# Q, K and V by the seven-product scheme at two levels instead of one, in a two-layer graph-attention kernel

## The chip, the core and the metric

The kernel runs on one core of one Trainium2 chip. The metric is the time of one execution on the device in microseconds (us), the median of several runs. Beside it stands one profiled execution with a trace of every instruction. The engines are named as the profile names them: PE is TensorE's matmul, PEld its weight load, DVE is VectorE, ACT is ScalarE, POOL is GpSimd, SP is the engine whose queue issues nearly all transfers.

## The reference

There are 128 batches of 128 tokens with 512 features, in float32, and a 128x128 mask of zeros and ones per batch. Two layers follow one another, each inside a residual and a normalisation:

```python
q = (x @ Wq + bq), k = (x @ Wk + bk), v = (x @ Wv + bv)      # 512x512 weights, 8 heads of 64
logits = einsum(q, k) / sqrt(64);  logits = where(adj > 0, logits, -1e9)
out = relu(einsum(softmax(logits), v) @ Wo + bo)
x = layernorm(x + out)
# layer 1
Wh = x @ W;  s_i = Wh @ a1;  s_j = Wh @ a2
e = leaky(s_i[:, None] + s_j[None, :]);  e = where(adj > 0, e, -9e15)
h = leaky(softmax(e, axis=1) @ Wh)
x = layernorm(x + h)
```

The five products with 512x512 weights (Wq, Wk, Wv, Wo, W) hold most of the arithmetic.

## The kernel before

**Tiling.** Batches go in groups of four (`GROUP = 4`, 512 tokens). Q, K and V are computed for a group at a time. Wo and W are applied to pairs of batches (256 tokens). Softmax and the second layer's attention go batch by batch.

**The seven-product scheme.** A product of two matrices cut into 2x2 blocks needs eight block products; Strassen's scheme, in the variant used here, needs seven and some sums of blocks. The weights' sums are made once at the start (`right_blocks`, L152 to L155). The sums of x are made on GpSimd (`left_blocks`, L276 to L279: xS per group for Q, K and V, oS and x1S per pair for Wo and W). For Q, K and V a block is 256 tokens by 256 features, so one product of blocks is four 128x128 weight loads, each with 256 columns streamed, on L367:

```python
for m in range(2):
    cols = slice(m * P, (m + 1) * P)
    for kc in range(2):
        lhs, rhs = xs[:, kc, cols], w[:, kc, :]
        if transposed_out:
            lhs, rhs = w[:, kc, cols], xs[:, kc, :]
        nc.tensor.matmul(p[:, m, :], lhs, rhs, start=..., stop=True)
```

A float32 product on PE shows as two records in the trace. The seven products p1 to p7 of one matrix go to three PSUM banks (y, w, x; `ps_st`, one buffer each) in an order that lets later products add to what earlier ones left in a bank:

```python
ORDER = (("p1", "t0"), ("p5",), ("p6", "t2"), ("p2", "c11"),
         ("p7", "t3", "c22"), ("p4", "c21"), ("p3", "c12"))
```

p1, p6, p7 and p4 all go to bank y. After p1, p6 and p7 ACT copies that bank out (t0, t2, t3: L344, or L348 where Q's bias is added), so p6 must wait for t0, and so on. c21 is a copy by ACT too. c11, c22 and c12 are sums on DVE of a bank and a copy (L385, 512 columns). Per matrix and group that is 7 products, 4 copies and 3 sums.

**The rest.** `scores` (L520) multiplies Q and K of one batch into two banks; DVE adds the mask (L534), takes the maxima (L543); ACT takes the exponentials (L554) and divides by the sums (L568). The attention matrix goes out to DRAM in `store` and comes back as 32-row stripes in `fetch` (L581), DVE transposes it in 32x32 blocks (L587), and `attend` (L600) multiplies by V. Wo and W follow in `pair_product` (L448), with copies on ACT (L459) and sums on DVE (L693, L697, L772, and residuals on L686). Normalisations take their statistics on DVE (L644, L646), a power on GpSimd (L650, L652) and are applied on DVE (L665). The second layer's attention is one product (L841). The scores e are turned by way of DRAM, too (`store_sender`, `fetch_sender`, L817 on DVE), and its softmax is scaled on DVE (L836).

**Weights.** The seven blocks of Wq and Wk stay in SBUF. Those of Wv are written to DRAM once and fetched again in every group (`wv_n`, 256 KB a block, seven per group, three buffers).

**Order.** Everything is issued in one program order, and each engine works through its own instructions in that order. A step `t` of the main loop is one batch. Even steps start the softmax of two batches and apply W to an older pair, odd steps finish the softmax and apply Wo. Between these pieces, `group()` issues the next product of Q, K or V, and `pair()` the next of Wo or W. So the order follows from the places of these calls in the loop. The last four batches follow an order written out by hand (`PLAN`). All transfers but four go through SP's queue, which works in order as well.

Of the kernel before, what the change touches and what calls it, by code (L numbers as in the profile page):

```python
# [17 lines left out]
GROUP = 4  # L18
# [3 lines left out]


@with_exitstack
def kernel(
# [16 lines left out]

# [28 lines left out]
    b_rows = small.tile([2 * NC, P], F32, name="b_rows", tag="e", bufs=1)  # L111
    b_cols = const.tile([P, 2, NC], F32, name="b_cols")

    def turn_biases():
        p_b = psum("p_b")
        nc.tensor.transpose(p_b[:, : 2 * NC], b_rows, ident[: 2 * NC, : 2 * NC])
        nc.vector.tensor_scalar_mul(b_cols[:, 0, :], p_b[:, :NC], QSCALE)
        nc.vector.tensor_copy(b_cols[:, 1, :], p_b[:, NC : 2 * NC])

# [44 lines left out]
    wq = const.tile([P, 7, 2, HALF], F32, name="wq")  # L164
    wk = const.tile([P, 7, 2, HALF], F32, name="wk")
    wo = const.tile([P, 7, 2, HALF], F32, name="wo")
    w1 = const.tile([P, 7, 2, HALF + 1], F32, name="w1")
    wv = dram.tile([7, P, 2, HALF], F32, name="wv", bufs=1)
# [3 lines left out]

    def load_wv():

        tiles = [big.tile([P, 2, 2, HALF], F32, name="wv_t", tag="v", bufs=3) for _ in range(3)]
        tiles.append(work.tile([P, 2, 2, HALF], F32, name="wv_t", tag="pa", bufs=2))
        t = [tiles[n // 2][:, n % 2] for n in range(7)]
        load_blocks(Wv, tiles[:2], nc.sync)

        def write(n):  # L180
            return lambda: nc.sync.dma_start(wv[n], t[PLACE[n]])

        ops = right_blocks(t)
        return [write(0)] + ops + [write(n) for n in (4, 5, 1, 6, 3, 2)]
# [5 lines left out]
    def load_w1():  # L190

        a_b = [work.tile([P, D], F32, name="a_b", tag="wh", bufs=4) for _ in range(2)]
# [5 lines left out]
        loads = [load_a(0), load_a(1)] + block_loads(W1, columns(w1), nc.sync)  # L198
# [34 lines left out]
    X, XT, XS, Q, K, V, MF, OT, X1T, X1, WH = ({} for _ in range(11))  # L233


    def spread(src):

        z = work.tile([P, 4, P], F32, name="xz", bufs=3)
        block = src.rearrange("(a i) (q e) -> q i a e", i=32, q=4)
        for q in range(4):  # L240
            nc.sync.dma_start(z[32 * q : 32 * q + 32], block[q])
        return z
# [8 lines left out]
    def load_x(b):  # L251
        X[b] = spread(x[b])

    def load_residual(b):

        X1[b] = work.tile([P, D], F32, name="x1", bufs=7)
        nc.sync.dma_start(X1[b], x[b])

# [6 lines left out]
    def sum_x(g):  # L265
        sums = big.tile([P, 3, 2, 2 * P], F32, name="xS")
        XS[g], ops = left_blocks(XT[g], sums)
        return lambda: [op() for op in ops]

# [71 lines left out]
    def copy_out(dst, p, o, bias):  # L341

        if bias is None:
            nc.scalar.copy(dst, p)  # L344
            return
        for m in range(2):
            col = bias[:, 2 * o + m : 2 * o + m + 1]
            nc.scalar.activation(dst[:, m, :], p[:, m, :], AF.Identity, bias=col)  # L348

    def group_product(g, turn, weight, out, transposed_out, bias=None):  # L350

        def bank(role):

            tag = "abc"[("ywx".index(role) - turn) % 3]
            return ps_st.tile([P, 2, 2 * P], F32, name=f"st_{role}", tag=tag)

        def multiply(p, n, start):
            w, xs = weight(n), XS[g][n]  # L360
            for m in range(2):
                cols = slice(m * P, (m + 1) * P)
                for kc in range(2):
                    lhs, rhs = xs[:, kc, cols], w[:, kc, :]
                    if transposed_out:
                        lhs, rhs = w[:, kc, cols], xs[:, kc, :]
                    nc.tensor.matmul(  # L367
                        p[:, m, :],
                        lhs,
                        rhs,  # L370
                        start=start and m == 0 and kc == 0,
                        stop=True,
                        skip_group_check=True,
                    )

        def read(name, p, o):
            t = work.tile([P, 2, 2 * P], F32, name=f"st_{name}")
            copy_out(t, p, o, bias)
            return t

        def add(h, o, p, t):
            if t is None:
                copy_out(out(h, o), p, o, bias)
            else:
                nc.vector.tensor_add(out(h, o), p, t)  # L385

        return strassen(bank, multiply, read, add)

    def products(g):

        for h in range(2):
            Q[g, h] = big.tile([P, NC, HALF], F32, name="qT", bufs=4)
            K[g, h] = big.tile([P, NC, HALF], F32, name="kT", bufs=3)
            V[g, h] = big.tile([P, 2, D], F32, name="v", bufs=3)

        def features_first(dst):
            return lambda h, o: dst[g, h][:, 2 * o : 2 * o + 2, :]

        def tokens_first(dst):
            return lambda h, o: dst[g, h][:, :, o * HALF : (o + 1) * HALF]  # L400

        ring, todo = {}, [0, 4, 5, 1, 6, 3, 2]

        def fetch():
            if todo:
                n = todo.pop(0)
                ring[n] = work.tile([P, 2, HALF], F32, name="wv_n", bufs=3)
                nc.sync.dma_start(ring[n], wv[n])

        pieces = [  # L410
            group_product(g, 3 * g, lambda n: wq[:, PLACE[n]], features_first(Q), True, b_cols[:, 0, :]),
            group_product(g, 3 * g + 1, lambda n: wk[:, PLACE[n]], features_first(K), True),
            group_product(g, 3 * g + 2, ring.pop, tokens_first(V), False),
        ]

        chains = [in_order(chain) for chain in pieces]

        def with_fetch(step, n=1):
            def run():
                step()  # L420
                for _ in range(n):
                    fetch()

            return run

        chains[1][0] = with_fetch(chains[1][0], 2)
        chains[2][0] = with_fetch(chains[2][0])
        chains[1][5] = with_fetch(chains[1][5])
        for n in (1, 2, 3):
            chains[2][n] = with_fetch(chains[2][n])  # L430

        order = [chains[0][n] for n in ((0, 3, 1, 2, 4) if g == 0 else range(5))]
        if g == 0:
            first = order[0]
            order[0] = lambda: (first(), other_half())
        order += [chains[1][0], *chains[0][5:], *chains[1][1:5]]
        order += [chains[2][0], chains[1][6], chains[1][5], *chains[2][1:5]]
        return order + chains[2][5:], pieces[2], fetch
# [427 lines left out]
    def on(b):  # L866
        return 0 <= b < B
# [370 lines left out]

# [176 lines left out]
```

## Time and profile before

| | value |
|---|---|
| median of 3 runs | 2357.7 us (2355.76 to 2360.14) |
| profiled execution | 2352.5 us, span of its instructions 2350.7 us |
| granted PE clock | 0.999 |
| instructions | 43613 |
| PE / PEld busy | 2324.7 us (99%) / 1978.8 us (84%) |
| DVE busy | 1706.9 us (73%) |
| ACT busy | 1506.7 us (64%) |
| POOL busy | 763.0 us (32%) |
| transfers | 395.28 MB, mean 168 GB/s, 54.4% of 16 DMA engines' time in the main queue |

In such a profile "busy" is the time in which at least one instruction of the engine runs, as a share of the span. A matmul's end is modelled, and matmuls overlap in the pipeline, so that a busy PE is not yet one that starts a matmul as often as it can: the distance from one start to the next tells that. A group row names line, engine, operation, output<-input, shapes, count, then busy time and the mean of one instruction, then the idle time before these instructions and what ended it. A timeline row gives start and length in us, engine, line, and how many alike instructions were merged.

### The profile page before, as it was taken

Reading aid. Unit: us, or ns where it says so; the run is one execution under the profiler, and the core shown is the slowest. Engines: PE = TensorE matmul, PEld = TensorE weight load, DVE = VectorE, ACT = ScalarE, POOL = GpSimd, SP = SyncE. Lnnn points to the kernel's source line nnn. Section 1 sums busy time; section 2 is a strip of 40 time slices with the busy share of each in tenths; the row PEclk is TensorE's granted clock in tenths of the full one; section 3 lists DMA queues with packets and bytes.
Section 4 is the critical chain, followed back from the end, with each engine's and each line's share of the span. In section 5 each row is a group of like instructions: output and inputs, shape, how many; then the busy total and the mean of one; then the engine's idle time right before and its main releaser. Section 6 shows DMA issues by size and latency. Waiting matters only on the chain.

```text
span 2350.7 us, 43613 instructions
## 1 busy us (share of the span) xinstructions
PE 2324.7 (99%) x13362; PEld 1978.8 (84%) x13362; DVE 1706.9 (73%) x3462; ACT 1506.7 (64%) x5459; POOL 763.0 (32%) x1191
## 2 busy tenths in 40 slices
PE   8999999999999999999999999999999999999998
PEld 7788888888888888888888888888888888888875
DVE  5677776777767777777777677677777776777767
ACT  3656656657666666566665666665766666657676
POOL 2232333323333323333233333333332333323326
PEclk9999999999999999999999999999999999999999
DMA  7655555555555555555555555555555555555454
GB/s 198 181 167 165 167 168 173 170 160 176 169 163 175 167 172 160 170 175 162 166 169 166 178 169 164 169 171 162 174 165 169 174 161 177 166 167 169 155 166 131
DMA packets 435561, 395.28 MB, mean 168 GB/s; under 512 B 108280, under 2 KB 339328, under 8 KB 435328
## 3 DMA queue, kind: packets, MB, share of 16 engines
q1 hardware_dynamic: 435008, 392.23, 54.4%
q8 instruction: 107, 1.75, 0.3%
q14 instruction: 126, 1.03, 0.1%
q10 hardware_dynamic: 320, 0.26, 0.0%
HBM read 248.58 MB, written 143.72 MB: 167 GB/s over the span
## 4 chain that ended last, share of the span: by engine, by line
PE 92%; DMA 3%; DVE 2%; ACT 1%; SPq 1%; issue 1%; POOL 0%; POOLq 0%; DVEq 0%; ACTq 0%
PE st_y L367 26%; PE p_y L448 18%; PE st_w L367 13%; PE p_w L448 9%; PE st_x L367 7%; PE lg L520 5%; PE p_oT L600 5%; PE p_h L841 4%; PE p_x L448 4%; DMA paz<-pa_dram 1%; DMA pa_dram<-pa 1%; ACT pa L568 0%; ACT pa L554 0%; SPq L581 0%; DMA e_dram<-e 0%
## 5 line engine op out<-in xcount | busy, mean ns | idle before, releaser
L650 POOL TENSOR_SCALAR ve<-mv 128x1 f32<-128x1 f32 x256 | 70.0, 273 | 1415.4 <-DVE mv L646 1409.7
L554 ACT ACTIVATE pa<-pa,nmax 128x128 f32<-128x128 f32 x1008 | 393.5, 394 | 2.6 <-DVE nmax L543 2.6
L568 ACT ACTIVATE pa<-pa,rs 128x128 f32<-128x128 f32 x1008 | 327.6, 397 | 0.7 <-DVE rs L564 0.6
L344 ACT COPY st_t<-st_y 128x512 f32<-128x512 f32 x192 | 111.2, 579 | 198.3 <-PE st_y L367 198.0
L459 ACT COPY pr_t<-p_y 128x257 f32<-128x257 f32 (+1 forms) x375 | 139.0, 371 | 125.1 <-PE p_y L448 120.7
L348 ACT ACTIVATE st_t<-st_y,b_cols 128x256 f32<-128x256 f32 x192 | 79.8, 466 | 202.3 <-PE st_y L367 202.3
L554 ACT ACTIVATION_READ_ACCUMULATOR pa<-pa,nmax 128x1 f32 x1008 | 192.5, 191 | 0.0
L587 DVE STREAM_TRANSPOSE pa<-paz 128x1024 f32<-128x1024 f32 x126 | 156.9, 1246 | 15.7 <-DMA paz<-pa_dram 14.1
L534 DVE TENSOR_TENSOR pa<-lg,mf 128x512 f32<-128x512 f32 x252 | 161.1, 680 | 1.1 <-PE lg L520 1.1
L614 ACT ACTIVATE oT<-p_oT,b_cols 128x128 f32<-128x128 f32 x504 | 137.1, 380 | 37.4 <-PE p_oT L600 37.3
L543 DVE TENSOR_REDUCE nmax<-pa 128x8 f32<-128x1024 f32 x126 | 151.7, 1204 | 2.2
L600 PEld LDWEIGHTS p_oT<-pa,v 128*64 128x64 f32 x2016 | 108.6, 137 | 51.7 <-issue 23.7
L652 POOL TENSOR_TENSOR rstd<-ve,mhalf 128x1 f32<-128x1 f32 x256 | 144.8, 566 | 21.3
L520 PE MATMUL lg<-kT,qT 64*128 64x128 f32 x2048 | 132.1, 279 | 0.0
L448 PE MATMUL p_y<-wo,oT 128*128 128x256 f32 x504 | 129.7, 380 | 1.2 <-ACT p_y L469 1.2
L520 PEld LDWEIGHTS lg<-kT,qT 64*128 64x128 f32 x2048 | 119.4, 188 | 12.3 <-issue 11.9
L448 PE MATMUL p_y<-w,x1T 128*128 128x257 f32 x496 | 128.4, 381 | 1.3 <-ACT wk L459 1.3
L448 PE MATMUL p_y<-wo,oS 128*128 128x256 f32 x504 | 129.5, 379 | 0.1
L600 PE MATMUL p_oT<-pa,v 128*64 128x128 f32 x2016 | 125.1, 276 | 4.5 <-DVE pa L587 3.9
L448 PE MATMUL p_y<-w,x1S 128*128 128x257 f32 x496 | 127.9, 380 | 0.0
L367 PE MATMUL st_y<-xT,wk 128*128 128x256 f32 x512 | 124.0, 385 | 0.0
L367 PE MATMUL st_y<-wv_n,xT 128*128 128x256 f32 x512 | 121.3, 380 | 1.5 <-ACT st_t L344 1.4
(197 smaller groups left out, 5726.9 us busy)
## 6 DMA issues: line engine op xcount, KB each, us to landing
pa_dram<-pa SPq DMA_DIRECT2D x126, 512.0 KB, 2.9
paz<-pa_dram SPq DMA_DIRECT2D x504, 128.0 KB, 2.8
wv_n<-wv SPq DMA_DIRECT2D x224, 256.0 KB, 3.0
x<-in_x_dram SPq DMA_DIRECT2D x128, 256.0 KB, 3.0
x_dram<-x SPq DMA_DIRECT2D x128, 256.0 KB, 2.4
xz<-x_dram SPq DMA_DIRECT2D x512, 64.0 KB, 2.0
xz<-in_x_dram SPq DMA_DIRECT2D x496, 64.0 KB, 2.2
out_dram<-z SPq DMA_DIRECT2D x120, 256.0 KB, 2.7
```

The source lines that it names most:

```text
L367: nc.tensor.matmul(p[:, m, :], lhs, rhs, start=start and m == 0 and kc == 0, stop=True, skip_group_check=True,)
L448: nc.tensor.matmul(p[:, :width], xs()[n][:, kc, :], w[:, PLACE[n], kc, :], start=start and kc == 0, stop=True, skip_group_check=True,)
L459: nc.scalar.copy(t[:, :width], p[:, :width])
L520: nc.tensor.matmul(self.lg[r][:, c, :], q[rows, c, cols], k[rows, c, cols], start=c == 0, stop=True, skip_group_check=True,)
L534: nc.vector.tensor_add(by_head[:, r * NC : (r + 1) * NC], self.lg[r].rearrange("p c (b k) -> p c b k", b=4), mf.unsqueeze(1).to_broadcast( ...
L543: nc.vector.tensor_reduce(self.nmax, by_head, AX.XY, ALU.max, negate=True)
L554: nc.scalar.activation(self.pa[:, :, h, :], self.pa[:, :, h, :], AF.Exp, bias=self.nmax[:, h : h + 1], accum_out=self.sums[:, h : h + 1],)
L568: nc.scalar.activation(self.pa[:, :, h, :], self.pa[:, :, h, :], AF.Copy, scale=self.rs[:, h : h + 1])
L587: nc.vector.transpose(self.paT.rearrange("p h (a i) -> p a h i", i=32), self.paz.rearrange("p a (h k) -> p a h k", k=32),)
L600: nc.tensor.matmul(self.oT[r * HD : (r + 1) * HD, c, :], v[:, h * HD : (h + 1) * HD], self.paT[:, r * NC + c, :], start=c == 0, stop=True, ...
L614: nc.scalar.activation(OT[pair][:, c, h * P : (h + 1) * P], self.oT[:, c, :], AF.Identity, bias=b_cols[:, 1, c : c + 1],)
L652: nc.gpsimd.tensor_tensor(self.r, ve, mhalf, ALU.pow)
```

## The change

Each of the seven products of 256-wide blocks is cut again into 2x2 blocks of 128x128 and done by seven products, so that Q, K and V take 49 products of 128x128 by 128x128 each where they took 28 of 128x128 by 128x256.

The inner seven products are done in two rounds, `ROUNDS = ((0, 1, 4, 2), (5, 3, 6))`. A "chain" c is one matrix in one round: six chains per group. A chain runs the outer order p1 to p7 as before, but each outer product is now four (or three) matmuls of 128 columns, each into its own quarter of the bank. Copies and sums of the outer scheme are done on those 512 or 384 columns at once, into `out_Q`, `out_K`, `out_V` or scratch `cells`; there are twice as many of them. When both rounds are there, `combine` does the inner scheme's sums in SBUF: per group Q takes ten adds, six of them half as wide, K and V seven each. The inner sums of x (s1 to s4, each as one add of 512 and one of 384 columns) are new, too; they are made from x's outer sums once per group. Most of these adds are on GpSimd, some on DVE.

```diff
-            for m in range(2):
-                cols = slice(m * P, (m + 1) * P)
-                for kc in range(2):
-                    lhs, rhs = xs[:, kc, cols], w[:, kc, :]
-                    if transposed_out:
-                        lhs, rhs = w[:, kc, cols], xs[:, kc, :]
-                    nc.tensor.matmul(p[:, m, :], lhs, rhs, ...
+            j = place_in_stream.get((c, f"p{n + 1}"))
+            if j is not None:
+                fetch_until(j + AHEAD)
+            operand = INNER[g][1]
+            for index, m in enumerate(ROUNDS[r]):
+                xs = operand(n, INNER_PLACE.index(m))
+                w = weight(n, m)
+                lhs, rhs = (xs, w) if name == "V" else (w, xs)
+                nc.tensor.matmul(p[:, index, :], lhs, rhs, ...
...
+    def combine(c, engine):
...
+        def op(dst, left, right):
+            def run(by=None):
+                (by or engine).tensor_add(*(t(n) for t, n in (dst, left, right)))
...
+        if c % 6 == 0:
+            ops = []
+            for h, src in enumerate((half(0), raw)):
+                d, s = ([(t, n) for n in range(4)] for t in (half(h), src))
+                ops += [op(d[2], s[2], s[0]), op(d[0], s[0], s[3]), op(d[1], s[1], d[2])]
+            return ops
+        if c % 2 == 0:
+            return [op(s[2], s[2], s[0]), op(s[0], s[0], s[3]), op(s[1], s[1], s[2])]
+        return [
+            op(s[3], s[1], m[0]),
+            op(s[1], s[1], m[1]),
+            op(s[2], s[2], m[0]),
+            op(s[2], s[2], m[2]),
         ]
...
+        ops = {
+            "s1": ("tensor_add", "s1", a21, a22),
+            "s2": ("tensor_sub", "s2", "s1", a11),
+            "s3": ("tensor_sub", a21, a11, a21),
+            "s4": ("tensor_sub", "s4", a12, "s2"),
+        }
```

All 49 blocks of Wq are in SBUF. Those of Wk and Wv are made at the start (Wk's on DVE, Wv's on GpSimd), written to DRAM, and fetched in every group but the first, one or two outer products at a time, three fetches ahead, into four buffers of 512 KB:

```diff
+            blocks = work.tile([P, 2, 4, P], F32, name="w_n", bufs=AHEAD + 1)
...
+            nc.sync.dma_start(blocks[:, : len(at), : 4 - r, :], src.rearrange("n p i f -> p n i f"))
```

To make room, Wo and W lie where Wk's blocks lay at first, and x, Wh, z and oT share one tile (`arena`). Some small transfers of two batches are merged into one (x, the mask, the residual, the senders of e).

From step 6 to the last four batches the loop's calls are replaced by four lists, one per kind of step, that name every piece in order. `h` issues the next outer product of Q, K or V, `a` and `d` the next waiting copy on ACT or sum on DVE of that scheme, `k` the next add of `combine` (with `.v` on DVE), `i` an inner sum of x; w and z are the products with W and Wo, f and s the two softmaxes, e and n the second layer. One of the four, and the loop's core:

```diff
+    2: """
+        n.residual f.scores s.scores h w.p1 f.add.1 f.add.0 w.p5 f.reduce s.add.1
+        e.turn_blocks w.t0 w.p6 g.apply.0 k.v k.v f.exp.6.7 f.exp.4.5 w.t2 e.add h k.v
+        s.add.0 d f.reciprocals.1 m.turn e.maxima n.stats w.p2 n.rstd w.p7 a f.exp.0.1 w.t3
...
+            elif name == "a":
+                if acts:
+                    acts.pop(0)()
+            elif name == "d":
+                if vecs:
+                    vecs.pop(0)()
+            elif name == "k":
+                if combos:
+                    combos.pop(0)(nc.vector if rest else nc.gpsimd)
+            elif name == "i":
+                inner_sum(g if t % GROUP else g + 1, rest[0][:2], rest[0][2:],
+                          nc.vector if rest[1:] else nc.gpsimd)
```

At the start, the first product waits for a part of Wq's and x's inner differences, made on DVE (`wq.first`, `wq.second`, `x_inner`), and the other parts follow in `other_half`. At the end, two chains of V instead of one are left for the hand-written order, with their seven adds. The program's matmuls for Q, K and V go from 2688 to 4704, its DVE instructions from 3448 to 4220, its GpSimd instructions from 1196 to 1754, and SP's transfers from 3021 to 2543.

## The prediction, on record before the changed kernel was run

> **What bounds the kernel now.** I read the page from the top: busy shares, then the chain that ended last, then the stretches by time, then single lines.
>
> ```profile
> PE 2324.7 (99%) x13362; PEld 1978.8 (84%) x13362; DVE 1706.9 (73%) x3462; ACT 1506.7 (64%) x5459; POOL 763.0 (32%) x1191
> ...
> PE 92%; DMA 3%; DVE 2%; ACT 1%; SPq 1%; issue 1%; POOL 0%; POOLq 0%; DVEq 0%; ACTq 0%
> PE st_y L367 26%; PE p_y L448 18%; PE st_w L367 13%; PE p_w L448 9%; PE st_x L367 7%; PE lg L520 5%; PE p_oT L600 5%; PE p_h L841 4%; PE p_x L448 4%; DMA paz<-pa_dram 1%; DMA pa_dram<-pa 1%; ACT pa L568 0%; ACT pa L554 0%; SPq L581 0%; DMA e_dram<-e 0%
> ```
>
> TensorE bounds it, and 46% of the chain (26 + 13 + 7) is the product of L367 that the change rewrites. A busy matmul row is not yet a full one, so I check the spacing of starts in the timeline (columns: start, length in us):
>
> ```profile
> 9.85 1.04 PE L942 MATMUL p_x<-ident,x_turned 128*128 128x128 f32 x8
> 10.72 1.46 PE L367 MATMUL st_x<-xT,wq 128*128 128x256 f32 x6
> ...
> 1205.76 1.89 PE L367 MATMUL st_y<-xS,wq 128*128 128x256 f32 x8
> 1207.49 1.02 PE L841 MATMUL p_h<-wh,att 128*128 128x512 f32 x2
> ...
> 1211.33 0.86 PEld L520 LDWEIGHTS lg<-kT,qT 64*128 64x128 f32 x14
> ```
>
> Eight records of 256 columns start within 1.73 us, 216 ns each. (A product of 128x128 by 128x256 is two records: 5376 in the trace for 2688 in the program.) Eight transposes, each with its own 128x128 load and 128 columns, start within 0.87 us, 109 ns each. The last line is seven pairs of loads: (0.86 - 0.19)/6 = 112 ns per pair, two halves of 64 rows, each load 188 ns long, each followed by 128 columns.
>
> Then one group of four batches. The GpSimd sum L276, once per group, starts 24 times from 315.9 to 1974.4: 72.1 us per group. Eight groups by engine (columns: window, length, then busy PE, PEld, DVE, ACT, POOL, clock, DMA share, GB/s):
>
> ```profile
> 400.00:976.80 576.80, 576.80 (x3329) 493.40 (x3328) 423.46 (x856) 372.70 (x1361) 186.62 (x288) 1.00 0.55 169
> ```
>
> Per group: DVE 52.9, ACT 46.6, POOL 23.3 us. PE has no slack, DVE has 19 us.
>
> **What the Trainium skill says.** "TensorE: Matmul & The Clock Gate", section "LDWEIGHTS (loading the stationary operand)": the load takes columns/1.2 ns, 107 ns for 128, whatever the rows; its "Step-by-step" part says that the next load runs under the matmul in flight. The trace agrees: 84% PEld lies beside 99% PE, and the 112 ns pair fits a hidden load. The same page's "Back-to-back issue gap" has pairs at 128 columns at 81 ns where a lone gap is 56: 25 ns of load can show. No row here does so. "SBUF — State Buffer", section "SBUF: two separate sides": a DVE instruction with two SBUF inputs or in a 2-port mode and a GpSimd one hold one port pair exclusively; the loser waits. "GPSIMD Engine Reference", "Performance versus the Vector engine": a GpSimd add takes 1.96 times the DVE's; the trace has 1.27 against 0.69 us. On the lock the trace agrees:
>
> ```profile
> 1211.89 0.72 POOL L276 TENSOR_TENSOR oS<-oT 128x256 f32<-128x256 f32 x1
> ...
> 1210.66 0.52 DVE L665 TENSOR_SCALAR x<-x,mv,rstd 128x512 f32<-128x512 f32 x1
> 1211.92 0.97 DVE L665 TENSOR_SCALAR x<-x,mv,rstd 128x512 f32<-128x512 f32 x1
> ...
> 17.02 1.75 DVE L155 TENSOR_TENSOR wq<-wq 128x512 f32<-128x512 f32 x1
> 21.67 0.69 DVE L155 TENSOR_TENSOR wk<-wk 128x512 f32<-128x512 f32 x1
> ```
>
> The same DVE instruction takes 0.52 us alone and 0.97 beside a GpSimd add; a two-input add 0.69 alone and 1.75 in the start, where GpSimd sums at the same time.
>
> **The change, part by part, per group.**
>
> 1. *PE.* Removed: 3 x 28 products, 168 records at 216 ns, 36.3 us. Added: 3 x 49 products of 128 columns, 294 records at 110 ns (between 109 and 112), 32.3 us. Saved: **4.0 us**; 72.1 becomes 68.1. If 25 ns of load show, 294 x 134 = 39.4, 3.1 lost. The loads double their share: a record then has a load for each 107 ns stream. I take 110, because both rows with a load per 128 columns show it.
>
> 2. *DVE.* Each product now ends in two rounds (four and three blocks), so nine more sums out of PSUM of 384 columns come. The inner combination adds six of 512 and three of 256 on DVE, and the inner sums of x three of 512 and three of 384. 512-column adds start 0.61 us apart (21.06 to 21.67), 256 columns take 0.42 less the same overlap of 0.08, 0.34; 384 between, 0.47. Sum: 9 x 0.47 + 9 x 0.61 + 3 x 0.34 + 3 x 0.47 = **12.1 us**. DVE 65.0 of 68.1: the cover that hid all its work is almost used up.
>
> 3. *GpSimd.* Thirteen adds of 512 (12 combining, one inner sum) at 1.3, three of 256 at 0.73, one of 384 at 1.0: 20 us more, 43 of 68. It has room itself. But the lock: DVE has 39 instructions per group of the kinds named (4 residual sums of z, 8 normalisations, 4 + 4 on att and mf, 4 residuals of layer zero, 15 of the new ones), and GpSimd adds cover 36 of 68 us. Met by chance and held 0.4 us each, that is 39 x 0.54 x 0.4 = 8.4 us. Before has some of it in its 52.9: the means of 639 and 871 ns for normalisations and 543 for att, against 0.52 and 0.29 alone, make 86 us, 2.7 per group. So +5.7 by chance; from 0 (the lists place them apart) to 13 (all meet). Below zero is excluded unless meetings fall under today's. I take 3.5: DVE 68.5.
>
> 4. *ACT.* Twelve more copies of 384 columns at some 0.38 (0.371 for 256 and 0.585 for 512, less 0.1 overlap), Q's bias in smaller pieces: +4.9, 51.5 of 68. Hidden.
>
> 5. *Transfers.* K and V come from DRAM: 98 blocks of 64 KB, 6.4 MB, where V alone was 1.8; 12.2 MB per group become 16.8 and the share 0.55 some 0.78 at worst, less if the larger packets go faster. A fetch holds 512 or 384 KB, landing in perhaps twice the 3.0 us of wv_n, and is issued three fetches, some five products or 8 us, ahead: hidden. SP issues in order; a fetch behind the store of pa waits for ACT's divisions, and x, adj and paz behind a fetch wait for a free one of four buffers. SP's transfers fall from 3021 to 2543, since pairs of small loads are merged. 0 to 1.5 us per group; I take 0 and keep 1.5.
>
> 6. *Orders as lists.* Moving steps costs nothing in itself, but each engine's queue is strict: a DVE sum that waits for PE holds the sums behind it, ACT's copies of p1 and p6 free the bank that the next product of four or three short matmuls (0.9 or 0.65 us, before 1.7) wants. Two engines at about 68 us that wait for each other do not both stay full: +1.2, between 0 and 5.
>
> 7. *Start.* Inner differences of Wq and x before the first products can end: about ten adds of 0.4 to 1.0 us, beside GpSimd: +6 us, 0 to 12. The end has two chains of V instead of one; its adds lie beside softmax: 0.
>
> Period: 68.5 + 1.2 = 69.7, 2.4 less than 72.1. Sum against the profiled execution: 2352.5 (span 2350.7 and 1.8 around it) - 32 x 2.4 + 6 = 2282. The median of the runs lies 5.2 above that execution: **2287 us**.
>
> **The rivals.**
>
> - *DVE and its lock become the bound; slower.* One mechanism, in the steady groups on DVE: 65.0 + 5.7 by chance, and 3 us idle for waits on PE and ACT, make 73.7, 1.6 over today: 2357.7 + 51 + 6 = 2415 us. It decides as soon as lock and idle time together exceed 7 us per group (72.1 - 65.0). For it: the sums leave 3 us, and DVE today waits 115 us for pr_t of ACT and 67 for p_w of PE. Against it: the combining work has a whole group to be done in and may be placed where DVE reads PSUM. 28 in 100.
> - *PE gets all of it.* DVE's sums fit beside PE, the lock is met no more than now: 2357.7 - 128 + 6 = 2236 us. 15 in 100.
> - *The load shows.* With 134 ns per record 3.1 us per group are lost, 2357.7 + 99 + 6 = 2463; at the full 190 ns of a load 294 x 0.19 = 55.9, about 2990. Against: the 109 and 112 ns above. 3 in 100.
> - *Gains and losses cancel*, within 0.2% (about 5 us, what runs of this kernel can tell from no change): 4 in 100.
>
> **The numbers.** Likeliest, 50 in 100: 2287 us, by itself 2250 to 2345. Faster 0.65 (50 + 15), same 0.04, slower 0.31 (28 + 3). The range runs from the PE case with a cheap start, 2230, to the lock case, 2415; it leaves out the visible load, the worst of the lock and the best corner.
>
> **What would show it.** Right: L367's successor at 109 to 112 ns per start with PEld near the whole span; DVE over 92% busy; GpSimd near 62%; DVE's two-input adds longer in the mean than 0.69 us; PE idle before products, released by DVE and ACT; groups some 69 to 70 us apart. Wrong: matmul starts over 120 ns apart with nothing awaited (step 1); DVE under 88% busy and PE full (steps 2 and 3 too dear); waits of PE on w_n (step 5); normalisations and new adds over 1 us in the mean and groups over 72 us apart (the first rival).

## The result, and the profile after

| | before | after |
|---|---|---|
| median | 2358.75 us (4 runs, 2355.76 to 2360.14) | 2584.31 us (4 runs, 2581.41 to 2593.21) |
| span of the profiled execution | 2350.7 us | 2579.6 us |
| maxima of the third group's first batch | 168.9 us | 236.8 us |
| one group of four batches, steady | 72.1 us | 77.6 us |
| from the 29th group's maxima to the end | 309.3 us | 325.4 us |

After/before is 1.0964 (95% interval 1.0934 to 1.0995): slower, where 2287 us and a faster kernel were predicted, and beyond the range's end of 2415. The third to fifth rows are read from DVE's reduction of the logits to their maxima (`nmax`), in each group that of its first batch; the steady value is the mean over the fifth to 29th group. The 229 us between the spans are 68 in the start, 145 in the 26 groups that follow, and 16 in the end.

The page of after, busy times and the chain that ended last (shares by engine, then by line):

```profile
PE 2313.3 (90%) x17394; PEld 2035.5 (79%) x17394; DVE 2170.0 (84%) x4234; ACT 1663.7 (64%) x5971; POOL 1504.3 (58%) x1749
...
DVE 34%; DMA 28%; PE 15%; ACT 10%; SPq 7%; issue 5%; POOL 1%; DVEq 0%; ACTq 0%; POOLq 0%
```

(SPq is SP's queue issuing transfers.) PE fell from 92% of the chain to 15%. No engine took its place: DVE is busy 84%, the DMA engines about 73% (see below). The chain hops between DVE, transfers and ACT; the reading here is that the length of such a chain of steps, and not one full engine, sets the period. PE itself works at the pace that was forecast (timeline of after; start, length):

```profile
1217.60 0.39 PE L578 MATMUL st_w<-xT,wq 128*128 128x128 f32 x2
1217.82 0.39 PE L578 MATMUL st_w<-inner_s,wq 128*128 128x128 f32 x2
...
1218.49 0.61 PE L578 MATMUL st_w<-inner_s,w_n 128*128 128x128 f32 x4
```

Eight records start within 0.89 us, 111 ns each, with wq and with streamed weights alike. What PE waits for in the steady stretch, here always 400 to 2300 us, of after (total, times, longest):

```profile
PE p_oT L896 <- DVE pa L883: 45.3, 40, 3.3
PE st_y L578 <- DVE out_Q L612: 33.6, 25, 1.4
PE st_x L578 <- DMA w_n<-wk: 23.9, 20, 2.6
PE st_y L578 <- ACT cells L591: 20.3, 25, 0.8
```

In the same stretch of before the sum of all PE's waits that the trace names is under 3 us; the longest of its lines is

```profile
PE st_y L367 <- DMA wv_n<-wv: 1.1, 1, 1.1
```

The first line of after ends a round trip: pa, the attention matrix, is stored to DRAM, fetched as stripes (paz), and transposed on DVE (L883). The page's list of transfers gives its legs (KB each, median us from issue to landing), those of before first, then those of after beside the new stream:

```profile
pa_dram<-pa SPq DMA_DIRECT2D x126, 512.0 KB, 2.9
paz<-pa_dram SPq DMA_DIRECT2D x504, 128.0 KB, 2.8
```

```profile
paz<-pa_dram SPq DMA_DIRECT2D x504, 128.0 KB, 3.2
pa_dram<-pa SPq DMA_DIRECT2D x125, 512.0 KB, 4.4
w_n<-wk SPq DMA_DIRECT2D x93, 512.0 KB, 4.8
w_n<-wv SPq DMA_DIRECT2D x93, 512.0 KB, 5.7
```

A mean share hides this. The steady stretch as a whole, then slices of 4 us of after (window, length, busy PE, PEld, DVE, ACT, POOL, clock, DMA share, GB/s) and PE's timeline in them:

```profile
400.00:2300.00 1900.00, 1745.06 (x13285) 1538.32 (x13284) 1633.53 (x3220) 1263.40 (x4568) 1124.68 (x1299) 1.00 0.73 216
```

```profile
1224.00:1228.00 4.00, 4.00 (x31) 3.79 (x30) 3.03 (x6) 3.86 (x15) 1.07 (x2) 1.00 0.94 251
1228.00:1232.00 4.00, 1.42 (x13) 1.26 (x13) 1.46 (x5) 2.49 (x8) 3.84 (x5) 1.00 1.04 234
1232.00:1236.00 4.00, 4.00 (x17) 3.41 (x16) 1.66 (x3) 0.37 (x1) 1.03 (x2) 0.60 0.92 297
```
```profile
1231.57 0.46 PE L578 MATMUL st_x<-xT,w_n 128*128 128x128 f32 x2 [2.58 <-DMA w_n<-wk]
...
1233.54 1.91 PE L742 MATMUL p_w<-wo_w,oS 128*128 128x256 f32 x4
...
1238.81 1.03 PE L742 MATMUL p_w<-wo_w,arena 128*128 128x256 f32 x4
```

For 12 us the DMA engines are full while the mean over the groups is 0.73. That is no rare case: of the 475 slices of 4 us in the steady stretch, 152 have a share of 0.90 or more, against 2 in the kernel before. PE waits 2.58 us for one fetch, the longest wait of that line, and then pays again: its clock falls to 0.60, and four records that take 1.03 us at full clock take 1.91. The second payment is rare in after: the clock was at half for 10 of the 1900 us.

### The profile page after: what moved, and what is told of

The parts are those of the page before. It is cut to its first block, busy times and chain, and to the rows that moved or that the text cites. A ratio compares the mean times of both kernels' runs of the same rounds, so it can differ in the third digit from the quotient of the medians.

```text
span 2579.6 us, 53024 instructions
## 1 busy us (share of the span) xinstructions
PE 2313.3 (90%) x17394; PEld 2035.5 (79%) x17394; DVE 2170.0 (84%) x4234; ACT 1663.7 (64%) x5971; POOL 1504.3 (58%) x1749
## 3 DMA queue, kind: packets, MB, share of 16 engines
q1 hardware_dynamic: 516064, 537.17, 70.5%
## 4 chain that ended last, share of the span: by engine, by line
DVE 34%; DMA 28%; PE 15%; ACT 10%; SPq 7%; issue 5%; POOL 1%; DVEq 0%; ACTq 0%; POOLq 0%
DMA paz<-pa_dram 12%; PE st_y L578 5%; DVE pa L883 4%; SPq L877 4%; PE p_y L742 4%; DMA x_dram<-arena 3%; DMA w_n<-wk 3%; DVE pa L830 3%; ACT pa L850 3%; DMA xz<-x_dram 3%; DVE arena L962 3%; DMA pa_dram<-pa 3%; DVE out_Q L628 3%; ACT pa L864 2%; DVE nmax L839 2%
## 5 line engine op out<-in xcount | busy, mean ns | idle before, releaser
L1156 ACT ACTIVATE arena<-p_h 128x512 f32<-128x512 f32 x120 | 71.6, 597 | 271.9 <-DMA out_dram<-arena 191.9
L883 DVE STREAM_TRANSPOSE pa<-paz 128x1024 f32<-128x1024 f32 x125 | 154.8, 1239 | 100.0 <-DMA paz<-pa_dram 97.2
L591 ACT COPY cells<-st_y 128x384 f32<-128x384 f32 x288 | 136.8, 475 | 121.2 <-DVE out_Q L628 65.6
L628 POOL TENSOR_TENSOR out_Q<-out_Q,cells 128x512 f32<-128x512 f32 x94 | 120.0, 1278 | 124.8 <-DVE cells L612 116.8
L896 PE MATMUL p_oT<-pa,out_V 128*64 128x128 f32 x2000 | 136.7, 279 | 61.5 <-DVE pa L883 60.3
L896 PEld LDWEIGHTS p_oT<-pa,out_V 128*64 128x64 f32 x2000 | 106.7, 136 | 103.2 <-DVE pa L883 75.4
L962 DVE TENSOR_SCALAR arena<-arena,mv,rstd 128x512 f32<-128x512 f32 x239 | 173.8, 727 | 13.4 <-POOL rstd L949 13.4
L941 DVE BATCH_NORM_STATS2 st<-arena 128x6 f32<-128x512 f32 x248 | 169.4, 683 | 1.3
L911 ACT ACTIVATE arena<-p_oT,b_cols 128x128 f32<-128x128 f32 x504 | 141.0, 377 | 35.2 <-PE p_oT L896 34.6
L628 POOL TENSOR_TENSOR out_K<-out_K 128x512 f32<-128x512 f32 x93 | 117.1, 1273 | 74.9 <-DVE out_K L612 61.9
L816 PE MATMUL lg<-out_K,out_Q 64*128 64x128 f32 x2048 | 139.0, 286 | 6.2 <-DVE out_K L628 6.0
L816 PEld LDWEIGHTS lg<-out_K,out_Q 64*128 64x128 f32 x2048 | 125.1, 194 | 18.8 <-issue 10.1
```

What stands on the lines that cost most here:

```text
L628: (by or engine).tensor_add(*(t(n) for t, n in (dst, left, right)))
L816: nc.tensor.matmul(self.lg[r][:, c, :], q[rows, 2 * (b % 2) + c % 2, c // 2, :], k[rows, 2 * (b % 2) + c % 2, c // 2, :], start=c == 0, st ...
L883: nc.vector.transpose(self.paT.rearrange("p h (a i) -> p a h i", i=32), self.paz.rearrange("p a (h k) -> p a h k", k=32),)
L896: nc.tensor.matmul(self.oT[r * HD : (r + 1) * HD, c, :], v[:, c % 2, c // 2, r * HD : (r + 1) * HD], self.paT[:, r * NC + c, :], start=c == 0,
L941: nc.vector.bn_stats(st, self.src)
L962: nc.vector.tensor_scalar(self.src, self.src, self.mv[:, 0:1], self.r, ALU.subtract, ALU.mult)
```

## The experiments

Names below say what was changed against the kernel after; the line numbers shift by a few. A kernel that leaves out work computes other values. Each ran beside the kernel before (medians 2352.5 to 2356.2 us in the batches). The last column is the start of the maxima of the third group's first batch, as above. Where an expectation gives this mark for a new kernel, it means that of the next batch, which is 3.3 us later in after (240.1 us) and 4.3 in start_free_no_combine.

| kernel | time, us | against before (95%) | steady group | third group at |
|---|---|---|---|---|
| after | 2584.3 | 1.0964 (1.0934 to 1.0995) | 77.6 | 236.8 |
| no_stream | 2445.6 | 1.0388 (1.0358 to 1.0419) | 72.7 | 236.3 |
| stream_unread | 2565.3 | 1.0897 (1.0855 to 1.0939) | 76.7 | 238.5 |
| unread_half | 2487.8 | 1.0559 (1.0516 to 1.0602) | 74.3 | 234.8 |
| unread_act | 2713.2 | 1.1516 (1.1456 to 1.1576) | 82.1 | 245.1 |
| no_combine_pool | 2511.7 | 1.067 (1.0609 to 1.073) | 75.2 | 230.2 |
| no_combine | 2509.2 | 1.0659 (1.0628 to 1.069) | 75.4 | 227.5 |
| no_stream_no_combine_pool | 2365.7 | 1.0038 (1.0022 to 1.0054) | 70.3 | 227.1 |
| no_stream_no_combine | 2345.7 | 0.9965 (0.9952 to 0.9979) | 70.1 | 212.7 |
| comb_pool | 2768.1 | 1.1748 (1.1657 to 1.1839) | 83.5 | 237.5 |
| comb_vec | 2597.6 | 1.103 (1.0995 to 1.1065) | 77.6 | 239.8 |
| ahead2 | 2730.7 | 1.1595 (1.1558 to 1.1633) | 82.0 | 251.4 |
| ahead2_z2 | 2728.1 | 1.1584 (1.1547 to 1.1621) | 81.9 | 251.6 |
| start_free | 2427.3 | 1.0302 (1.026 to 1.0344) | 72.6 | 219.3 |
| start_free_no_combine | 2324.4 | 0.9865 (0.9829 to 0.9901) | 70.0 | 196.7 |
| start_dve | 2577.8 | 1.094 (1.0909 to 1.0972) | 77.6 | 231.9 |
| start_late_stores | 2573.2 | 1.0927 (1.0879 to 1.0974) | 77.6 | 228.0 |
| before_stream | 2746.2 | 1.1668 (1.1554 to 1.1781) | 85.2 | 197.5 |

### The stream

**No fetches.** In `weight`, K's and V's chains from the second group on read Wq's blocks, and nothing is fetched (V's chains of the last group read sums of x instead):

```diff
-            return ring[c, f"p{n + 1}"][:, (0, 1, 2, 0, 3, 1, 2)[m], :]
+            return wq.inner(m)[:, PLACE[n], :]
...
-            if j is not None:
+            if j is None and j is not None:      # never true: no fetch is issued
                 fetch_until(j + AHEAD)
```

> Left out: all fetches of w_n. From the second group on K's and V's products read Wq's resident blocks (the last group's V reads x's own sums), so those values are other ones; all matmuls, copies, sums and adds stay as they are. Transfer theory (the streamed blocks, 4.6 MB more per group, share the queue and the engines with the round trips of pa, x and e, so DVE's transposes and with them PE get their data late): the group falls from 77.3 us to 71 or less, the time to some 2400 us, and DVE's wait for paz falls from 97 us to under 30. Lock theory (DVE and GpSimd block each other on their shared SBUF port, and DVE's sums come late): at most 1 us per group, 2555 us or more.

139 us go, 4.9 per group, and the start stays where it was. Landings fall back, and the chain is PE's again (page of no_stream, then a line of PE's waits and the whole steady stretch):

```profile
PE 64%; DVE 22%; DMA 6%; ACT 3%; SPq 2%; issue 2%; POOL 1%; DVEq 0%; ACTq 0%; POOLq 0%
...
paz<-pa_dram SPq DMA_DIRECT2D x504, 128.0 KB, 3.0
pa_dram<-pa SPq DMA_DIRECT2D x125, 512.0 KB, 2.8
```
```profile
PE p_oT L896 <- DVE pa L883: 6.2, 13, 1.2
```
```profile
400.00:2300.00 1900.00, 1825.59 (x14159) 1636.05 (x14159) 1725.59 (x3425) 1342.96 (x4858) 1189.26 (x1386) 1.00 0.48 142
```

142 GB/s for 72.7 us are 10.3 MB per group, less than the 12.2 of before, because V's own fetches of 1.8 MB are gone too. So 4.9 us are the price of the whole stream of 6.4 MB, not only of the 4.6 MB that the change added.

**Fetched, but unread**: the other operands alone, with every fetch issued as in after. Now PE never waits for w_n, and a fetch never waits for PE to free a buffer.

> As the run without fetches (same replaced operands), but every fetch of w_n is still issued at its place and lands; nothing reads it, so a fetch waits for no matmul and no matmul waits for a fetch. Transfer theory in its traffic form (bytes and packets ahead of the round trips): within 1.5 us per group of the changed kernel, 2540 us or more. In its queue form (SP stands still before a fetch until PE has freed a buffer, and all transfers behind it stand too): near the run without fetches, 2400 to 2450 us. Lock theory: no difference to the changed kernel beyond 20 us in either run.

Only 19 us come back. Waiting for the blocks and for their buffers is thus a small part; the traffic is 120 of the 139. By which way the bytes act is shown only in part. Of the 4.9 us per group, PE's waits for pa hold 1.6 (45.3 us against 6.2 in the stretch) and those for w_n 1.0; the rest lies in smaller waits and in a PE that is busy 1.4 us longer per group, and was not assigned.

**Fewer bytes, in as many transfers** (two inner blocks of each three or four, so four sevenths of the bytes, although the expectation says half):

```diff
-            nc.sync.dma_start(blocks[:, : len(at), : 4 - r, :], src.rearrange(...))
+            nc.sync.dma_start(blocks[:, : len(at), :2, :], src.rearrange(...)[:, :, :2, :])
```

> The stream of blocks is issued as in the kernel with unread fetches (2565 us, 76.6 us per group), but each fetch brings two of the three or four inner blocks, so half of the bytes of 512 KB fetches, in as many transfers. If the bytes on the DMA engines delay pa's round trip, about half of the 120 us between 2565 and 2446 (no fetches) goes: 2500 to 2510 us, 74.5 per group. If the number of transfers that SP issues in order counts, it stays within 10 us of 2565.

77 of the 120 us go with three sevenths of the bytes, and SP's issues are unchanged: it is the bytes. That the saving is more than in proportion fits engines that are full at times (slices with a share of 0.90 or more fall from 158 to 75 of 475), but was not tested further.

**The unread stream from another queue**: `nc.scalar.dma_start` for `nc.sync.dma_start`.

> The unread stream, its fetches issued by ACT instead of SP: another queue, the same bytes. If SP's order is the cost (pa's loads stand behind fetches in one queue), 2450 to 2480 us. If the DMA engines' share is the cost (transfers of both queues share them), 2550 to 2570 us; ACT has 25 us per group free, so issuing 16 fetches there adds at most 1 us.

Slower than either theory said, by 148 us against the same stream on SP. The legs of pa, counted from their own issue, did not get shorter when the stream left SP's queue, but longer (page of stream_unread, then of unread_act; PE's wait for pa in the steady stretch rose to 114 us, from 37.5):

```profile
paz<-pa_dram SPq DMA_DIRECT2D x504, 128.0 KB, 3.2
pa_dram<-pa SPq DMA_DIRECT2D x125, 512.0 KB, 4.5
```

```profile
paz<-pa_dram SPq DMA_DIRECT2D x504, 128.0 KB, 3.8
pa_dram<-pa SPq DMA_DIRECT2D x125, 512.0 KB, 5.0
```

This agrees with the Trainium skill, "DMA: Bandwidth & Descriptors", section "Issuing engines are not separate DMA queues": transfers of all issuing engines run on the same 16 DMA engines and interleave. It is no clean comparison of two queues, though, and does not by itself rule SP's order out. A fetch takes 0.42 us of ACT's queue in the mean, and 370 of them in the steady stretch make 6.7 us per group, where the expectation allowed 1. PE's clock was at half for 150 of the 1900 us, against 17 in stream_unread. How the 148 us divide among these was not separated.

**Fetch distance, and the z row.** ACT's longest wait in after is for the store of the single z row (L1156, 165 us in the steady stretch), so it was a suspect. Giving up one fetch buffer makes room for a second row:

```diff
-    AHEAD = 3
+    AHEAD = 2        # ahead2; w_n has AHEAD + 1 buffers
     def z_slot():    # ahead2_z2
-        return cut(AFTER_WH, D)
+        z_turn[0] ^= 1
+        return z_more if z_turn[0] else cut(AFTER_WH, D)
```

> Fetches are issued two ahead instead of three, with three buffers instead of four; bytes and transfers stay. If the distance matters, PE waits for w_n more than today's 26 us of the steady groups: up to 2 us per group, 2640 us. If the bytes on the engines are what counts, within 15 us of 2584.

> As the kernel with fetches two ahead, and in the room this frees a second row for z, so that ACT need not wait for the store of the last one (165 us in 25 groups, 6.6 per group). If that wait is how the stream's bytes reach the time, the group loses 2 to 4 us: 2470 to 2530 us. If pa's round trip through DVE is the way, ACT's wait vanishes and the time stays within 15 us of the one with a single row.

The second row is worth 3 us, within what the two intervals leave open, so with fetches two ahead that wait (177 us there), though the largest on ACT's list, was on no path: without it ACT waits 194 us for PE's p_oT instead. With three ahead it was not tested. The distance, which I took for nearly indifferent, is worth 146 us: two ahead is too late (waits of PE, steady stretch of ahead2). PE's clock, at half for 116 of the 1900 us against 10 in after, has a part in the 146.

```profile
PE st_y L578 <- DMA w_n<-wk: 65.5, 23, 4.2
PE st_x L578 <- DMA w_n<-wv: 63.8, 23, 3.7
```

With three ahead PE's waits for w_n are some 24 us in the same stretch. A longer distance was not tried; stream_unread, in which nothing waits for a block, suggests that it would bring back some 19 us.

**The same traffic in the kernel before.** Nine copies per group of two of Wv's blocks, DRAM to DRAM, issued after products of Q and K; nobody reads them:

```diff
+                t = dram.tile([2, P, 2, HALF], F32, name="unread", bufs=3)
+                nc.sync.dma_start(t, wv[0:2])
```

> The kernel before, with nine unread copies of two of Wv's blocks (512 KB each, from DRAM to DRAM) added per group from the second on, 4.6 MB as in the changed kernel, issued by SP after products of Q and K. If bytes cost time only where the group has no slack (before, PE waited 3 us for pa in a whole run), the time stays within 10 us of 2357. If they cost as much here as there, 4.6 us per group: 2490 to 2510 us. Half of that would say that both count.

I had come to think that the bytes hurt only because the new kernel has no slack. That falls: the old one loses 13 us per group, at a mean DMA share of 0.66. The same lines say how in part (page, and PE's waits in the steady stretch, of before_stream):

```profile
pa_dram<-pa SPq DMA_DIRECT2D x126, 512.0 KB, 6.0
paz<-pa_dram SPq DMA_DIRECT2D x504, 128.0 KB, 2.9
```
```profile
PE p_oT L613 <- DVE pa L600: 156.2, 44, 7.1
```

The copies also write to DRAM and stand in other places than the fetches of after, so 13.1 and 4.9 us are not a ratio of the kernels. The wait for pa is 7.0 of the 13.1 us per group; besides, PE's clock was at half for 191 of the 1900 us, and never there in the kernel before.

### The adds of the inner combination

**Without GpSimd's adds, without any** (the traffic stays), and **the same without fetches**: `op` in `combine` returns without its add if it is GpSimd's, or always (then Q's second half is set to zero once instead).

> Left out: the inner scheme's adds (combine) that GpSimd does, twelve of 512 and three of 256 columns per group; those on DVE stay. Lock theory: DVE's two-input adds fall from means of 0.9 to 1.6 us to 0.7, DVE saves 5 us or more per group, the group falls to 72 us or less, the time to 2430 us. Transfer theory: 1 to 2 us per group at most, 2530 us or more, with DVE still waiting some 90 us for paz.

> Left out: all adds of combine, on both engines (DVE nine per group). A 1024-column memset at the start gives Q's never written half a value. Lock or DVE-load theory: DVE has 6 us per group less to do besides, 70 us per group, 2370 us. Transfer theory: not over 3 us per group in all, 2490 us or more.

> Left out: the fetches (Wq's blocks are read instead) and GpSimd's adds of the combination; DVE's adds of it stay. Without fetches a group takes 72.6 us, without any of the adds 70.15. If GpSimd's part (the lock) holds the difference, 70.2 to 70.8 us per group, 2350 to 2375 us; if DVE's own 8 us of adds hold it, 72 to 72.5, 2410 to 2440 us.

> Left out: the fetches of K's and V's blocks from the second group on (these chains multiply by Wq's blocks), and all adds of the inner combination. If transfers and lock are two separate costs, their savings add: from 2584 us the 139 of the fetches and the 75 of the adds go, 2370 us, groups 70 to 70.5 us apart. If both only delay the same chain (DVE's transposes of pa), the second saving is small: 2420 to 2445 us, 72 us per group. Below 2320 us would say that PE's 68 us per group are reached and the start's 70 us are gone too.

GpSimd's adds are worth 73 us with the stream and 80 without; with DVE's left out as well, 75 and 100. So stream and adds are two costs that add up, nearly all of the adds' steady cost is GpSimd's, and without both a group takes 70.1 us, close to the 69.3 (68.1 + 1.2) that the forecast has without its lock. The mechanism shows in one instruction (timeline of no_stream; start, length):

```profile
1199.23 0.66 DVE L630 TENSOR_TENSOR out_V<-out_V,cells 128x512 f32<-128x512 f32 x1
...
1200.89 2.68 POOL L630 TENSOR_TENSOR out_V<-out_V,cells 128x512 f32<-128x512 f32 x2
1200.95 1.49 DVE L962 TENSOR_SCALAR arena<-arena,mv,rstd 128x512 f32<-128x512 f32 x1 [0.46 <-POOL rstd L949]
1202.36 1.75 DVE L630 TENSOR_TENSOR out_V<-out_V,cells 128x512 f32<-128x512 f32 x1
...
1205.59 0.65 DVE L614 TENSOR_TENSOR out_Q<-st_x,out_Q 128x512 f32<-128x512 f32 x1
```

GpSimd adds out_V from 1200.89 to 1203.57; in that time the same add takes 1.75 us that took 0.66 before. L614, which reads PSUM, keeps its 0.65, but it stands behind the others in DVE's queue, and PE waits 1.34 us for it, once in each group: the second line of PE's waits above. In no_stream_no_combine_pool that line has shrunk (first no_stream, then without GpSimd's adds):

```profile
PE st_y L580 <- DVE out_Q L614: 35.2, 27, 1.4
```
```profile
PE st_y L580 <- DVE out_Q L614: 0.8, 2, 0.5
```

DVE's busy time per group is 66.0 us in no_stream and 62.4 with GpSimd's adds gone: the lock that the Trainium skill tells of ("SBUF — State Buffer", "SBUF: two separate sides") costs DVE 3.6 us per group and the period 2.4. Leaving GpSimd's adds out also removes every wait for their results; in no_stream neither PE nor DVE has such a wait among its longest, so the lock is the reading that fits.

**All adds to GpSimd, nearly all to DVE** (steady lists; thirteen adds per group moved in comb_vec, GpSimd keeps two):

```diff
-                    combos.pop(0)(nc.vector if rest else nc.gpsimd)
+                    combos.pop(0)(nc.gpsimd)                                          # comb_pool
+                    combos.pop(0)(nc.vector if rest or t % GROUP != 1 else nc.gpsimd)  # comb_vec, and three k of list 1 as k.v
```

> All adds of the inner combination in the steady groups go to GpSimd: nine a group (six of 512 columns, three of 256) move from DVE, where they take 8.0 us per group. If DVE's load is what the adds cost, DVE falls from 84% and the group from 77.2 to 75 us: 2520 us. If the lock is the cost (more GpSimd adds to meet, GpSimd up by 10 us a group), the group goes to 78 to 80 us: 2605 to 2670 us.

> In the steady groups all of GpSimd's adds of the combination but two go to DVE, some ten of 512 or 256 columns, 0.61 or 0.34 us each when alone, 5.5 us per group. If the lock is what they cost (DVE's instructions lose 3.5 us per group to it, 65.9 busy against 62.4), DVE stays near 68 busy of 77 and the group gets shorter by 1 to 2 us: 2525 to 2555 us. If DVE's queue is the cost, it gets longer: 2600 us and more.

comb_pool lost 184 us, far more than was expected of the lock. GpSimd is only 63% busy, but takes 1.3 us where DVE takes 0.68, and the one `cells` buffer is not free until the adds have read it (DVE's waits in the steady stretch of comb_pool):

```profile
DVE cells L612 <- POOL out_Q L628: 93.2, 23, 4.1
```

PE's clock was at half here, too, for 137 of the 1900 us; its part of the 184 us was not separated.

comb_vec missed as well: the gain expected did not come. Its adds are free of the lock (groups of DVE's L628, first after, then comb_vec; count, busy, mean ns),

```profile
L628 DVE TENSOR_TENSOR out_Q<-cells 128x256 f32<-128x256 f32 x50 | 40.9, 856 | 0.0
```
```profile
L628 DVE TENSOR_TENSOR out_Q<-cells 128x256 f32<-128x256 f32 x48 | 18.1, 418 | 0.0
```

but DVE now works 70.5 us per group instead of 66.7, and the group stays at 77.6. In this kernel the adds cost about the same on either engine.

### The start

In the kernel after PE first waits 8.03 us for the inner differences. Then DVE sums Wk's blocks while GpSimd sums Wv's, each keeping the other waiting, and a sum out of PSUM (L612) that PE needs stands behind DVE's: 6.30 us (timelines of after):

```profile
30.86 1.64 DVE L159 TENSOR_TENSOR wo_w<-wo_w 128x512 f32<-128x512 f32 x1
...
35.88 2.03 DVE L190 TENSOR_TENSOR wo_w<-wo_w 128x896 f32<-128x896 f32 x1
37.84 0.68 DVE L612 TENSOR_TENSOR cells<-st_w,cells 128x512 f32<-128x512 f32 x1
```
```profile
23.33 1.39 PE L578 MATMUL st_w<-inner_s,wq 128*128 128x128 f32 x4 [8.03 <-DVE inner_s L397]
...
38.57 0.80 PE L578 MATMUL st_w<-xT,wq 128*128 128x128 f32 x2 [6.30 <-DVE cells L612]
```

From 20 to 40 us PE is busy 9.29 us, at a clock of 0.59.

**start_free**: no_stream without the 16 sums and 8 stores of Wk's and Wv's blocks (the first group reads Wq's too). **start_free_no_combine**: without the combination's adds as well.

```diff
-    chores += wk.build(nc.vector) + wk.stores(...)
-    chores += wv.build(nc.gpsimd) + wv.stores(...)
```

> As the kernel without the fetches (2446 us), and for the first group K and V use Wq's blocks too, so that the 16 sums of Wk's and Wv's blocks and the eight stores of them go. The third group's maxima come at 240 us in the kernel after as in the one without the fetches, 71 later than before. If these sums and stores cost the start its time, that point moves to 175 to 190 us and the time to 2380 to 2395 us. If it is the longer first chains (DVE's and GpSimd's new adds within every group, with nothing yet to overlap), it moves by less than 15 us: over 2430 us.

> Left out: fetches, the sums and stores of Wk's and Wv's blocks (Wq's are read), and all adds of the inner combination. If weights (18 us) and adds (23 us) are separate parts of the start's 71 us, the third group's maxima come at 199 us and the time is 2327 us; what then lies over the 169 of before, 30 us, belongs to the short products waiting for copies and adds that stand behind softmax in the queues of ACT and DVE. If both are one and the same wait, 215 us and 2345 us.

The first went against its theory: the third group comes 17 us earlier than in no_stream, not 50 to 65. The second hit, at 201.0 us in its count and 2324.4: sums and stores are worth 17 us, adds 24, both together 40, so they hardly overlap. Of the other 28 us, 13 lie before the first maxima (55.3 us against 42.3), where PE's longest waits are for DVE's inner differences (6.7) and sums of Wq (3.4), 10 in the second group (67.6 us long against 57.4) and 5 in the third. That short products wait there for copies and adds behind softmax is read from the timeline, and was not tested. The traces show one part more: PE's clock was at half for 38 of these 197 us (51 of the 237 in after), and never in this stretch in the kernel before. PE was busy for 25.6 of the 38 us, so by an estimate from these numbers its work took some 13 us longer than at full clock.

**start_dve**: `wv.build(nc.vector)`; **start_late_stores**: besides, all stores after all sums.

> Only the start changes: the eight sums of Wv's blocks go from GpSimd to DVE, so that Wk's sums on DVE (1.63 to 1.75 us for 512 columns beside GpSimd, 0.69 alone) run without it. If the lock holds the start there, Wk's eight sums end some 8 us earlier and Wv's eight follow in as much: third group's maxima at 232 to 240 us against 240, 2575 to 2585 us. If DVE's queue itself is what PE waits for, it comes 5 to 10 us later: 2590 us.

> As the kernel that builds Wv's blocks on DVE (2578 us), with the eight stores of Wk's and Wv's blocks issued after all 16 sums. If the stores ahead of the mask's load hold the first softmax, the first maxima come at 60 to 66 us instead of 73 and the time falls to 2560 to 2570. If the sums on DVE hold it, within 5 us of 2578.

5 us and 4 us of the third group's time. The first maxima come at 73.4 and 72.3 us, so the stores did not hold them. The second has the lowest median of the kernels that compute everything in the new scheme, 11 us under after; none of these beats the kernel before.

## Why the prediction was wrong, point by point

- *1, PE: right.* 110 ns were taken, 111 to 112 are seen; PE is busy 69.0 us per group in no_stream_no_combine, forecast 68.1. No weight load shows.
- *2 and 4, DVE and ACT: right within some per cent.* DVE 62.4 us without the GpSimd adds against 65.0, ACT 51.4 (no_stream) against 51.5.
- *3, the lock: right for DVE, mis-sized for the period.* 3.6 us measured, 3.5 taken. But I let it count only as far as DVE's sum rose over PE's, 0.4 us. GpSimd's adds cost 2.4: a lengthened add delays the PSUM reader behind it, and that one holds PE's next product, however idle DVE is on the whole.
- *5, transfers: the step that failed most.* 0 taken, 1.5 at most, 4.9 measured for the whole stream. The bytes were right (16.8 MB per group forecast; 216 GB/s for 77.6 us are 16.8). The step asked whether a fetch arrives in time for PE, and who stands behind it in SP's queue while it waits for a free buffer; stream_unread has neither wait and gains only 19 us. What the bytes do to the landings of other transfers while they are in flight had no term, and pa's round trip is in a chain. A share of 0.78 at worst was read as room. No rival carried this, either; of the signs named, only PE's waits on w_n pointed at the stream.
- *6, strict order: about right.* 1.2 taken; PE is idle 1.1 us per group in no_stream_no_combine.
- *7, the start: failed.* 6 taken, 12 at most, 68 measured. I counted the first inner differences, and left out that the second-level sums of Wk and Wv (17 us) and the combination (24 us) fall in a stretch that has no other work to lie beside. The other 28 us, in which the halved clock has a part, stay open.
- *The first rival* named the lock, but by a full DVE. DVE never filled: 84%. Its 2415 us lie 31 under no_stream (2446), and come by another sum: they have 1.6 us more per group than before and 6 for the start, no_stream has 0.6 and 67.

The sum of what was measured, 70.1 + 2.6 (adds) + 4.9 (stream), is the 77.6 us of after. Against the forecast of 69.7 that is 7.9 us more per group: 4.9 for the stream, 2.2 for the adds, 0.8 for PE and the order. The end's 16 us were not examined; they are gone in no_stream_no_combine (306.2 us from the 29th group on).

## What to carry to other kernels

Before calling added traffic hidden, list the transfers that lie in a chain of waits and ask what their landings become while the new bytes are in flight; a mean share below one was no answer here. When a bound engine is relieved, work out the chain that comes next (here store, fetch, transpose, product), and price a slowed instruction by who stands behind it, not by its engine's busy sum. Count a start apart: here little there covered the added work.

## What the runs showed of the hardware

- A wait can cost PE twice. After 2.58 us without work the clock was 0.60 in a slice of 4 us, and four records took 1.91 us instead of 1.03. Of the ten times PE stood idle for 1.8 us or more in the steady stretch of after, three (2.3, 2.6 and 3.3 us) were followed by half the clock for 3.4 us; one of 3.1 us was not. In unread_act, with idle times up to 5.3 us, it was 27 of 28. The Trainium skill, "TensorE: Matmul & The Clock Gate", "Part 1: The HAM clock gate", has half the clock after at least one idle window of about 3.4 us; here shorter waits were followed by it.
- 6.4 MB more per group lengthened the landing of a 512 KB store from 2.8 us (no_stream) to 4.4, and 4.6 MB of DRAM-to-DRAM copies to 6.0 from 2.9, at mean shares of 0.73 and 0.66.
- An add on DVE with both inputs in SBUF took 1.75 us beside GpSimd's adds and 0.66 before them; one that reads PSUM kept its 0.65.
- Issuing a fetch of 384 or 512 KB took 0.42 us of ACT's queue in the mean (unread_act).
